# Eight heads' value products at once in the last cross attention, and an earlier normalisation in its feed-forward

## The chip, the cores and the metric

The kernel runs on one core of one Trainium2 chip. The metric is the device time of one execution in microseconds (us); the time before is the median of three runs, 4806.71 us (4796.98 to 4807.12). The core's engines run side by side, each in the order of its own instructions: TensorE (PE; its weight loads are listed as PEld), VectorE (DVE), ScalarE (ACT), GpSimd (POOL), and SyncE (SP), which issues the DMAs here. They wait for each other through semaphores. TensorE writes its results to PSUM, a small memory of banks; DVE and ACT bring them from there to SBUF, the working memory.

## What is computed

Four layers work on x, 32 samples of 112 rows by 256, with a context of 375 rows per sample:

```python
x = _L0_xattn_ref(x, ctx, ...)       # cross attention, 16 heads of 64
x = _L1_xattn_ref(x, ctx, ...)       # quantised self and cross attention, gated feed-forward
x = _L2_xattn_ref(x, ctx, ctx, ...)  # cross attention, feed-forward
x = _L3_xattn_ref(ctx, x, ...)       # self attention, cross attention, feed-forward
```

The change touches the second and third step of the last layer:

```python
h = _mha(_ln(x, ln2_g, ln2_b), x_e, cq_w, ..., causal=False)   # x_e is the context
x = x + h @ c_proj_w + c_proj_b
h = relu(_ln(x, ln3_g, ln3_b) @ f_w1 + f_b1) @ f_w2 + f_b2     # 256 -> 1024 -> 256
return x + h
```

`_mha` has 16 heads of 16: scores q·k over 375 context rows, softmax, times the values, heads side by side.

## The kernel before

**Sweeps.** The layers are cut into nine sweeps over the 32 samples: `l0x`, `l1s`, `l1x`, `l1f`, `l2x`, `l2f`, `l3s`, `l3x`, `l3f` (the digit is the layer; s is self attention, x cross attention, f feed-forward). Two sweeps often run interleaved. In the last stage these are `l3x` and `l3f`: `l3f` follows `l3x` by a few samples and takes x from it on chip (`beside`). The end of `l3s` lies beside the start of `l3x`.

**Units and slots.** A unit of `l3x` is one sample with eight slots, one for two heads (`pair`, in `unit16`). A unit of `l3f` is a pair of samples with eight slots, one for each 128 columns of the hidden layer (`unitff`). `order` lays the slots of all sweeps in one list by planned times (`SPAN`, `DELAY`); `run` goes through it. Each slot has up to five steps, and `LAGS` says how many slots of its own sweep later each step comes. For a slot of `l3x`:

- `a`, at once: the scores of both heads (L1166, PE, to PSUM tiles `sc`, of which there are three), the maximum (L640, DVE), the exponential with its sum (L646, ACT) into a `k3` tile in SBUF.
- `r`, one slot later: the reciprocal of the sum (L680, DVE) and the scaling (L219, POOL, two instructions).
- `b`, three slots later: three transposes for each head (L698, PE, to `ps` tiles), and their copies to another `k3` tile, one on ACT (L202), one on DVE (L204).
- `c`, four slots later, only in every second slot: `av`, the products with the values for the four heads of the last two slots (L1130, PE; 12 matmuls, which the profile shows as 24). Four heads are called a quad below. Eight heads share one PSUM tile, allocated with the first quad and moved to SBUF after the second, with the bias, by ACT (L224) or DVE (L228) and DVE (L1150).
- the last slot's fifth step: the output projection (L237 to L239, "ps<-w,ot") and the sum with x (L1267, DVE).

Every product that must keep float32 accuracy is made as three matmuls of high and low halves, L237, L238 and L239 (`mm3`). The halves are cut with a copy (L202, L204 or L206) and a subtraction (L233).

A slot of `l3f` makes an up projection (`up`, L237 to L239, "ps<-h,w"), the ReLU with bias on ACT (L224, "s<-ps"), the high half on ACT (L202, "ot<-s"), the low half on POOL or DVE (L233, "ot"), and one slot later the down projection into one PSUM tile for the unit (L237 to L239, "acc<-w,ot"). The bias goes into that tile first (L291).

**Buffers.** The tag `k3` has 11 buffers: softmax outputs, transposed probabilities, loaded values, and the projected queries of `l3x` ("k<-ps,vec_L_xattn_cq_b", L224 and L976) while they are stored to memory (dq_l3x) and read back in another layout. PSUM holds four tiles `ps`, three `sc` and one `acc`. A tile whose buffers are all in use waits for the last reader of one of them.

**Atoms.** What a unit needs beforehand are atoms: small functions with a lead, in slots of their sweep, before the unit's first slot (`LEAD`). For a layer norm (`norm_atoms`) these are `load`, `stats` (L460 to L462 on DVE, L435 on POOL) and `apply` (L475 on DVE and POOL, transposes L477 on PE, L213 or L215, L202/L204/L206 and L233). Projections are atoms too and are spread by `fill` over the slots.

**The order on the engines.** `run` gives an order of issue, which the framework's scheduler then changes by its own estimates and by priorities: `av` of the unquantised sweeps is issued within `high_priority(offset=400)`, which lets it move ahead.

Of the kernel before, what the change touches and what calls it, by code (L numbers as in the profile page):

```python
# [61 lines left out]
class Kern:  # L62
# [12 lines left out]
        l3x=[0, 1, 3, 4, 4],  # L75
        l3f=[0, 4, 1, 4, 3],
# [8 lines left out]
        l2f=dict(load=6, stats=5, apply=3),  # L85
        l3s=dict(load=10, stats=8, apply=7, q=7, qload=3, k=6, v=3, c2=7, k2=1, v2=1),
        l3x=dict(load=16, stats=11, apply=10, cload=13, cut=12, q=9, qload=4, k=8, v=6, kload=8, vload=4),
        l3f=dict(load=3, stats=3, apply=2),
    )

    EARLY = 4
    HORIZON = dict(l0x=8, l1s=8, l1x=11, l1f=11, l2x=16, l2f=1, l3s=19, l3x=14, l3f=9)
    PARTS = dict(l0x=3, l1s=3, l1x=3, l1f=6, l2x=3, l2f=3, l3s=2, l3x=1, l3f=4)
    SCTAG = dict(l1x=("ps1", "sc"), l3x=("sc", "sc"))
    TWICE = ()

    SHARE = {
        ("l0x", "copy"): (1, 0, 0), ("l0x", "xn"): (0, 1, 2), ("l0x", "ohi"): (0, 1, 0), ("l0x", "prob"): (0, 1, 7),
# [959 lines left out]
    def unit16(self, s, b0, i, gb, g, wd, quant, self_attn, qb, kb, vb, dl, gvec, bvec):  # L1058
# [56 lines left out]
        def av(heads, pt, first, octets, ahead=True):  # L1115

            if first:
                st["av"] = self.ps([128, 2, S])
            o = st["av"]

            turn = list(enumerate(heads))
            if ahead and nb > 1:
                turn = turn[2:] + turn[:2]
            with self.tc.high_priority(offset=400) if ahead else nullcontext():
                for a in range(nb):
                    for n, hd in turn:
                        r = hd % 4
                        oc = hd // 8 if both else 0
                        odd = hd // 4 % 2
                        nc.tensor.matmul(  # L1130
                            o[32 * r : 32 * r + 32, oc, :],
                            st["v"](a, hd),
                            pt(a, n),
                            start=a == 0 and odd == 0 and oc == 0,
                            stop=a == nb - 1 and odd == 1 and oc == both,
                            tile_position=(0, 32 * r),
                        )
            if octets:
                if octets[0] == 0:
                    st["ot"] = self.t([128, 2, 2, S], F32R, "ot")  # L1140
                oc = slice(octets[0], octets[-1] + 1)
                hi, lo = st["ot"][:, 0, oc, :], st["ot"][:, 1, oc, :]
                o = o[:, : len(octets), :]
                if quant:
                    self.scale("ohi", hi, o, dl["so"])
                    nc.vector.scalar_tensor_tensor(lo, o, dl["so"], hi.bitcast(F32), ALU.mult, ALU.subtract)
                else:
                    bi = vb[:, octets[0] : octets[0] + 1]
                    self.shift("ohi", hi, o, bi)
                    nc.vector.scalar_tensor_tensor(lo, o, bi, hi.bitcast(F32), ALU.add, ALU.subtract)  # L1150

        def pair(pr):
# [38 lines left out]
            def c():  # L1191
                if m == 0 or qd % 2 == 0 and s in self.TWICE:
                    return
                for qq in (qd - 1, qd) if s in self.TWICE else (qd,):
                    heads, ocs = range(4 * qq, 4 * qq + 4), [qq // 2] if qq % 2 else []
                    if quant:
                        with self.tc.issue_after(self.mark[s].ins):
                            av(heads, lambda a, r: st["pt", qq][: blocks[a][1], 3 * r + a, :], qq % 2 == 0, ocs, False)
                    else:
                        av(heads, lambda a, r: st["pt", qq, r // 2][:, r % 2, a * S : (a + 1) * S], qq % 2 == 0, ocs)  # L1200
# [3 lines left out]
        def quad(qd):  # L1204
# [39 lines left out]
            def c():  # L1244
# [5 lines left out]
                st["pt", qd] = pt  # L1250
                if qd % 2 == 0 and s in self.TWICE:
                    return
                for qq in (qd - 1, qd) if s in self.TWICE else (qd,):
                    av([8 * (qq // 2) + qq % 2 + 2 * i for i in range(4)], lambda a, n: st["pt", qq][:S, n, :], qq % 2 == 0, [qq // 2] if qq % 2 else [])
# [414 lines left out]
```

## Time and profile before

| what | value |
|---|---|
| median of three runs | 4806.71 us (4796.98 to 4807.12) |
| profiled execution, its own time | 4799.79 us |
| its span, first to last instruction | 4797.7 us |
| busy share of the span: PE, PEld, DVE, ACT, POOL | 93%, 83%, 75%, 71%, 44% |
| mean granted clock of PE | 0.968 |
| last stage: one pair of samples (`l3x` and `l3f`) | 44.85 us |
| first score of `l3x`; last value product of `l3x` | 3996.5 us; 4771.7 us |

The profile is one execution. A group of rows has a line of the code, an engine, what is written and read, a count and times. "Idle before" names what ended a wait. A granted clock of 1.00 is full speed of TensorE. Matmuls overlap, so their length is longer than the step from one to the next; steps are read from start times.

### The profile page before, as it was taken

To read this page: it belongs to the slowest core of one execution; us is meant where nothing else is said; L and a number is where in the kernel's file an instruction comes from. 1 tells how busy PE (TensorE), PEld (TensorE's weight loads), DVE (VectorE), ACT (ScalarE), POOL (GpSimd) and SP (SyncE) were. 2 spreads that over 40 slices of the span, in tenths; PEclk is the share of its full clock that TensorE was granted. 3 is DMA by queue.
4 is the path that set the end of the run, shared out by engine and by line. 5 is a ranking of instruction groups with operands and counts; after the bars stand their busy time and mean duration, and the time that the engine had idled before them with its cause. 6 is when DMAs were issued, how large, how long until landed. Compare 5 with 4: busy or idle time off the path is not lost.

```text
span 4797.7 us, 111165 instructions
## 1 busy us (share of the span) xinstructions
PE 4449.6 (93%) x37824; PEld 3960.6 (83%) x37824; DVE 3619.7 (75%) x9803; ACT 3412.9 (71%) x10645; POOL 2131.3 (44%) x3676
## 2 busy tenths in 40 slices
PE   7999999998778999999999999999999997899999
PEld 6888888887667888887999999998899986778888
DVE  5788888888888888887688888888566655677776
ACT  5788888887767777775577777775555554677776
POOL 5455455556444343333233333334444443566665
PEclk9999999999889999999999999999999997899999
DMA  4433333334665565566355445543777777666663
GB/s 109 125 87 88 82 86 82 83 84 120 139 132 136 147 144 147 145 153 160 108 144 144 138 140 140 146 142 103 198 218 220 221 201 207 159 165 166 164 166 84
DMA packets 590020, 674.50 MB, mean 141 GB/s; under 512 B 331488, under 2 KB 499664, under 8 KB 589264
## 3 DMA queue, kind: packets, MB, share of 16 engines
q1 hardware_dynamic: 589456, 667.38, 54.6%
q8 instruction: 305, 5.00, 0.5%
q14 instruction: 259, 2.12, 0.1%
HBM read 323.55 MB, written 173.02 MB: 104 GB/s over the span
## 4 chain that ended last, share of the span: by engine, by line
PE 42%; DVE 5%; DMA 4%; ACT 1%; issue 1%; POOL 1%; SPq 0%; ACTq 0%; DVEq 0%; POOLq 0%
PE ps L698 7%; PE ps L237 6%; PE ps L238 5%; PE ps L239 5%; PE sc L807 3%; PE ps L829 3%; PE ps L1130 3%; PE sc L1166 2%; PE acc L237 2%; PE acc L239 1%; PE acc L238 1%; PE ps L1294 1%; DVE sm L640 1%; PE ps L1240 1%; DMA k<-k 1%
## 5 line engine op out<-in xcount | busy, mean ns | idle before, releaser
L219 POOL TENSOR_SCALAR k<-k,sm 112x375 f32<-112x375 f32 (+1 forms) x1536 | 941.7, 626 | 1054.1 <-DVE sm L680 474.5
L202 ACT ACTIVATE k<-ps 125x336 f32<-125x336 f32 (+4 forms) x2005 | 916.3, 470 | 419.8 <-PE ps L239 185.2
L640 DVE TENSOR_REDUCE sm<-sc 112x1 f32<-112x375 f32 x1792 | 945.1, 539 | 150.7 <-PE sc L807 86.6
L646 ACT ACTIVATE k<-sc,sm 112x375 f32<-112x375 f32 x1536 | 881.9, 580 | 103.3 <-DVE sm L640 79.9
L698 PE MATMUL ps<-ident,k 112*125 112x112 f32 x4608 | 736.4, 278 | 20.4 <-issue 4.0
L698 PEld LDWEIGHTS ps<-ident,k 112*125 112x125 f32 x4608 | 653.5, 191 | 76.0 <-issue 45.7
L807 PE MATMUL sc<-k,qs 128*112 128x376 f32 x2048 | 540.7, 357 | 21.4 <-ACT k L646 11.4
L237 PE MATMUL ps<-w,k 128*125 128x256 f32 (+2 forms) x1344 | 426.3, 317 | 32.0 <-ACT k L646 17.4
L729 DVE TENSOR_TENSOR k<-ps,k 64x376 fp32r<-64x376 f32 x640 | 350.3, 547 | 121.7 <-ACT k L202 106.5
L237 PE MATMUL ps<-h,w 128*128 128x224 f32 x1408 | 408.8, 297 | 34.6 <-DVE h L204 13.0
L204 DVE COPY k<-ps 125x336 f32<-125x336 f32 (+2 forms) x619 | 289.7, 468 | 152.3 <-PE ps L239 60.2
L238 PE MATMUL ps<-h,w 128*128 128x224 f32 x1408 | 394.0, 282 | 2.6 <-POOL h L233 2.0
L239 PE MATMUL ps<-h,w 128*128 128x224 f32 x1408 | 393.2, 282 | 1.3 <-POOL w L233 1.2
L238 PE MATMUL ps<-w,k 128*125 128x256 f32 (+2 forms) x1344 | 385.6, 287 | 0.0
L239 PE MATMUL ps<-w,k 128*125 128x256 f32 (+2 forms) x1344 | 384.7, 286 | 0.0
L829 PE MATMUL ps<-k,k 125*64 125x112 f32 (+1 forms) x4608 | 351.9, 297 | 1.6 <-ACT k L202 1.3
L215 POOL TENSOR_SCALAR k<-k,sm 112x375 f32<-112x375 f32 x256 | 165.8, 648 | 416.8 <-DVE sm L680 314.9
L237 PE MATMUL ps<-k,w 128*128 128x376 f32 x896 | 336.5, 376 | 15.2 <-ACT k L646 5.8
L807 PEld LDWEIGHTS sc<-k,qs 128*112 128x112 f32 x2048 | 305.3, 177 | 50.7 <-ACT k L646 24.9
L237 PEld LDWEIGHTS ps<-w,k 128*125 128x125 f32 (+2 forms) x1344 | 258.8, 193 | 82.5 <-ACT k L646 30.3
L646 ACT ACTIVATION_READ_ACCUMULATOR k<-sc,sm 112x1 f32 x1536 | 323.7, 211 | 0.0
L237 PEld LDWEIGHTS ps<-h,w 128*128 128x128 f32 x1408 | 272.4, 197 | 56.8 <-issue 18.2
(216 smaller groups left out, 12559.6 us busy)
## 6 DMA issues: line engine op xcount, KB each, us to landing
qs<-h SPq DMA_DIRECT2D x512, 224.0 KB
k<-k SPq DMA_DIRECT2D x192, 376.0 KB
k<-cd SPq DMA_DIRECT2D x64, 752.0 KB
vd<-k SPq DMA_DIRECT2D x128, 375.0 KB
k<-vd SPq DMA_DIRECT2D x128, 375.0 KB
qs<-dq_l3s SPq DMA_DIRECT2D x128, 224.0 KB
qs<-dq_l3x SPq DMA_DIRECT2D x128, 224.0 KB
x<-xd SPq DMA_DIRECT2D x224, 112.0 KB
```

The source lines that it names most:

```text
L202: self.nc.scalar.activation(out, in_, AF.Identity)
L204: self.nc.vector.tensor_copy(out, in_)
L219: self.nc.gpsimd.tensor_scalar(out, in_, by, 1.0, ALU.mult, ALU.mult)
L237: mm(out, lhs(0), rhs(0), start=start, stop=False)
L238: mm(out, lhs(0), rhs(1), start=False, stop=False)
L239: mm(out, lhs(1), rhs(0), start=False, stop=stop)
L640: nc.vector.tensor_reduce(nms[j], sc[j][:, :n], AX.X, ALU.max, negate=True)
L646: nc.scalar.activation(p[:, j, :n], sc[j][:, :n], AF.Exp, bias=nms[j], scale=1.0 if scale is None else scale, accum_out=sm[:, j : j + 1])
L698: self.nc.tensor.transpose(pst[:TB, a * S : (a + 1) * S], p[:, j, a * TB : (a + 1) * TB], self.ident[:S, :S])
L729: nc.vector.tensor_tensor(ks[o, j, :], pk[r, :TE], ks[r, j, :].bitcast(F32), ALU.subtract)
L807: nc.tensor.matmul(sc[:, :TE], qs[:, hd, q, bs], kk, start=q == 0, stop=q == 1)
L829: nc.tensor.matmul(o if gqa else o[:, mm, :], vq[:, a, hd * 64 : hd * 64 + 64], st["pt"][:, :, j, ta] if gqa else st["pt", mm][:, j, ta], ...
```

## The change

Two class constants change. `TWICE` makes step `c` of `l3x` return in the slot of the first quad and issue both quads' products in the slot of the second, two slots (four heads) later; the PSUM tile for the eight heads is then allocated there as well, and the first quad's transposed probabilities are kept until then. `LEAD["l3f"]` puts loading, statistics and application of the feed-forward's layer norm one slot of `l3f` earlier. Nothing else changes; the same instructions are issued.

```diff
-        l3f=dict(load=3, stats=3, apply=2),
+        l3f=dict(load=4, stats=4, apply=3),
...
-    TWICE = ()
+    TWICE = ("l3x",)
```

The code that reads `TWICE`, in `pair` (not changed):

```python
            def c():
                if m == 0 or qd % 2 == 0 and s in self.TWICE:
                    return
                for qq in (qd - 1, qd) if s in self.TWICE else (qd,):
                    heads, ocs = range(4 * qq, 4 * qq + 4), [qq // 2] if qq % 2 else []
                    ...
                        av(heads, lambda a, r: st["pt", qq, r // 2][:, r % 2, a * S : (a + 1) * S], qq % 2 == 0, ocs)
```

## The prediction

> **What bounds the kernel now.** I read the busy shares by slice first. TensorE (PE) is busy 93% of the span; the last five slices of 120 us, where most of the change lies, hold 9 at full clock. DVE and ACT stay at 6 and 7 there.
>
> ```profile
> PE   7999999998778999999999999999999997899999
> ...
> PEclk9999999999889999999999999999999997899999
> ```
>
> Then the stretches of the last stage, one per pair of samples. Columns: stretch and length in us, busy time of PE, its weight loads, DVE, ACT and POOL, granted clock, DMA share, GB/s.
>
> ```profile
> 4369.00:4414.00 45.00, 41.65 (x478) 36.76 (x477) 34.16 (x101) 33.86 (x109) 28.02 (x44) 1.00 0.70 170
> 4414.00:4459.00 45.00, 42.13 (x449) 36.99 (x452) 32.95 (x97) 32.10 (x103) 29.61 (x45) 0.96 0.65 164
> ```
>
> The pattern repeats every 44.85 us (the stall below stands at 4423.30, 4468.67, 4513.05). PE idles some 3.2 us per pair, and in every second pair the clock is granted at 0.96. PE bounds the stage. So a gain must come from fewer or cheaper PE instructions or from less waiting, and a loss from more waiting.
>
> The waits of PE alone, 4150 to 4700 us (total us, times, longest):
>
> ```profile
> PE sc L1166 <- ACT k L646: 9.6, 27, 1.3
> PE acc L237 <- ACT ot L202: 8.0, 13, 0.6
> ...
> PE ps L1130 <- ACT k L202: 2.8, 3, 1.3
> ```
>
> The 13 in the second row are the 13 pairs: once per pair the feed-forward's down projection (acc, L237) waits 0.61 us for the ReLU chain. The timeline of PE shows why, and what switching to the value products (L1130) costs (start, length, then what):
>
> ```profile
> 4393.14 0.48 PE L698 MATMUL ps<-ident,k 112*125 112x112 f32 x3
> 4393.39 0.40 PE L1166 MATMUL sc<-k,qs 128*112 128x376 f32 x1
> 4393.63 0.48 PE L698 MATMUL ps<-ident,k 112*125 112x112 f32 x3
> 4394.04 0.78 PE L1130 MATMUL ps<-k,k 125*32 125x112 f32 x24
> 4394.75 0.43 PE L1166 MATMUL sc<-k,qs 128*112 128x376 f32 x1
> ...
> 4407.45 0.28 PE L239 MATMUL acc<-w,ot 128*112 128x256 f32 x1
> 4407.66 0.38 PE L1130 MATMUL ps<-k,k 125*32 125x112 f32 x2
> 4407.97 0.58 PE L698 MATMUL ps<-ident,k 112*125 112x112 f32 x3
> 4408.48 0.78 PE L1130 MATMUL ps<-k,k 125*32 125x112 f32 x22
> 4409.19 0.58 PE L698 MATMUL ps<-ident,k 112*125 112x112 f32 x3
> 4409.53 0.40 PE L1166 MATMUL sc<-k,qs 128*112 128x376 f32 x1
> ```
>
> Three transposes (L698) before a score (L1166) take 0.25 us from start to start; before value products 0.41. A group of 24 takes 0.71, the score after it 0.27 instead of 0.24. One group's way in and out costs 0.41 - 0.25 + 0.03 = 0.19 us. A group split around transposes is dearer: from 4407.57 (the L239 before it steps by 0.12) to 4409.53 are 1.96 us for 24 products and 6 transposes, against 0.71 + 0.25 + 0.25 = 1.21: 0.75 us of overhead.
>
> **The change, part by part.** The program does the same arithmetic; only the order moves. All of it lies after 4000 us. In the built order, one steady pair (12 of them) has, for its eight quads of heads: before, 10 or 11 groups of value products, 2 or 3 of them splits; after, 4 or 5 groups and no split.
>
> *Value products for eight heads.* Overhead before: 2.5 splits x 0.75 + 5.5 whole groups x 0.19 = 2.9 us. After: 4.5 x 0.19 = 0.85. PE saves 2.1 us a pair, 12 x 2.1 = 25 us. The run-in beside l3s goes from 45 to 30 groups, but PE is only 72% busy in 4000 to 4100 and waits for DMAs there, so I count 15 x 0.19 = 3 us at most and take 2; the last pairs have 8 groups fewer, about 2 us. Sum: -29 us, -4 of it outside the 12 pairs.
>
> *What the later products displace.* The early half of the products was what PE did between an up projection and the down projection that needs its ReLU. Cover is measured as PE time between the two in the built order, at the row lengths above. Before, one of eight has 0.49 us of cover (two scores) and the rest 1.3 us or more; the short one waits 0.61, so the chain needs 1.10 us:
>
> ```profile
> 4422.18 0.51 PE L1166 MATMUL sc<-k,qs 128*112 128x376 f32 x2
> 4423.30 0.37 PE L237 MATMUL acc<-w,ot 128*112 128x256 f32 x1 [0.61 <-ACT ot L202]
> ...
> 4430.00 0.41 PE L238 MATMUL ps<-h,w 128*128 128x224 f32 x1
> 4430.21 0.41 PE L239 MATMUL ps<-h,w 128*128 128x224 f32 x1
> ```
>
> After, three in a row are short, just after the query projection of the next pair: 0.49; 0.49 in eight pairs, 0.98 or 1.34 in four; 0.98 in eight, 0.49 to 0.73 in four. Filled up to 1.10, the two new ones wait 0.43 + 0.24 us on the mean. The low half also needs POOL (L233, 0.66 us, starting when ACT ends). In the old short case a score stands between; in the new ones mostly two matmuls of 0.11 each, leaving 0.66 - 0.22 + 0.05 (a semaphore's delay: ACT's L202 ends at 4423.25, PE starts at 4423.30) = 0.5 us, once and a half per pair. Together +1.4. The low end is 0, if the chain starts earlier than its order suggests; the high end 2 x (0.61 + 0.5) = 2.2.
>
> *Banks and buffers behind the query projection.* With the products gone from there, six transposes follow at once and wait for PSUM: the second set for ACT's copy, which is third on ACT (0.35 + 0.44 us after the first L224), the last set for the ReLU (0.45). I get 0.6 + 0.5 us. In the same place before, PE waits 1.27 (L1166 <- L646, at 4477.07) or 0.8 to 1.3 (L1130 <- L202), so this is 0, between -0.3 and +0.3. What is queued behind on ACT is the next softmax, priced next.
>
> *The probabilities kept longer.* Four transposed tiles now live until the eighth head's, in the same 11 k3 buffers. In the built order a softmax output (L646) now takes the buffer of the second half of the queries, and so waits for its store. That store is slow in one period:
>
> ```profile
> 4251.40 0.44 DVE L976 SCALAR_TENSOR_TENSOR k<-ps,vec_L_xattn_cq_b,k 128x224 fp32r<-128x224 f32 x1
> 4256.73 0.45 ACT L202 ACTIVATE k<-ps 125x336 f32<-125x336 f32 x1 [0.79 <-DMA dq_l3x<-k]
> ```
>
> From 4251.84 to 4256.73 are 4.9 us; in the pair at 4477 nothing waits for it. Before, a copy of the probabilities waited for it, and PE lost 0.3 (L698 <- L202). Behind the exponential on ACT's queue stand a copy, three more exponentials and the ReLU, and behind those PE's scores, for which only three banks exist. At 4.9 us ACT is stopped some 1.6 us longer, and PE loses as much. At the fast end the exponentials still stand behind the ReLU pair (0.45 + 0.39) with nothing else for PE to score: about 0.4. I take the middle, +1.0 a pair, between 0.4 and 1.6.
>
> *Clock.* Clusters of idle time are followed by half clock: after 4422 to 4429 (2.7 us idle) the same L237 matmuls step by 0.21 us instead of 0.11, for 3.4 us, costing 1.7. Other pairs, with 3.5 us idle but spread over 9, have none. The new waits stand directly behind this cluster. I take 0.6 of a dip more per pair; PE would wait anyway in some 30% of it, so 0.6 x 1.7 x 0.7 = +0.7, between 0 and 1.7. [...]
>
> *Feed-forward normalised one slot sooner.* Its transposes stand at 4400.15 and the unit's bias matmul at 4414.28; the up projection that reads the result comes no earlier than 4410. It is ahead already, so moving it by one slot (44.85 / 8 = 5.6 us) wins nothing. No DMA is added: the loads of x go through memory no more than before, as the pair hands x over on chip. On POOL it moves L435 and L475 (0.72 + 1.33 us) ahead of one softmax scaling (L219, 1.17); the transposes of that scaling come some 4 us later, which hides it. If that cover is gone: 2 us a pair, taken as 0.
>
> Sum per pair: -2.1 + 1.4 + 0 + 1.0 + 0.7 = +1.0, times 12 is +12. Outside the 12 pairs -4, and +2 for the run-in, whose built order shows the same short covers. In all +10 us. The profiled execution took 4799.79 us (span 4797.7), 6.9 below the median of 4806.71; two of three runs lie at 4807. So 4809.8 beside the profiled one, 4817 beside the median, +0.2%.
>
> **The rivals.** (1) *Faster: the switches count and the waits do not.* The saved issue time appears in any case, while each wait can shrink: ACT and DVE are idle 25% here. It decides where the added waits and dips stay below 2.1 us a pair. With half of them (1.55): -0.55 x 12 - 3 = -10, 4797; with none: -29, 4778. Against it: the short covers are plain in the order, and the 0.61 recurs 13 times unchanged.
> (2) *Same: they cancel.* No further dips and the store at its fast end: (-2.1 + 1.4 + 0.4) x 12 - 2 = -6; with the middle store +2: 4801 to 4809. For it: pairs with 3.5 us idle and no dip.
> (3) *Clearly slower: all at their upper ends*, -2.1 + 2.2 + 0.3 + 1.6 + 1.7 = +3.7, times 12 less 2 is +42: 4849. For it: the rows of 4256.73 and 4430.00. Against: most pairs do not show the slow store.
> (4) *The change does nothing.* For the products the order refutes it; for the feed-forward it is my forecast.
>
> **How the numbers follow.** Three runs of one kernel span 10 us, so 0.2% (9.6 us) is about what can be told from no change. Forecast, slower by 0.2 to 0.6%: 0.38. Rival 1: 0.29. Rival 2, within 0.2%: 0.22. Rival 3: 0.11. Slower altogether 0.49. The sum stands just at the edge between slower and same, so either sign is open; I give 4817. The range leaves out the lowest part of rival 1 and half of rival 3: 4783 to 4846. The forecast alone has 4816 to 4835.
>
> **What would show it.** Right: pairs longer than 44.85 us; the row L237 <- ACT ot L202 with two to three times 13 waits, and a new PE row waiting for POOL L233; groups of 48 L1130 and no split; more stretches with a clock of 0.96 or less. Wrong if pairs take 43 us or less with the waits near 3.2 us, or if PE waits chiefly for the feed-forward's normalisation, or for value loads.

## The result

The changed kernel takes 4827.08 us (median of 8 runs, 4818.45 to 4841.52) against 4805.51 us (median of 8 runs, 4796.98 to 4815.97): ratio 1.0050, 95% interval 1.0039 to 1.0061. It is 0.5% slower. The forecast was slower by 0.2 to 0.6%, and the time lies in the range. The sign and the size came out, but by luck: the experiments show that the loss came from a step that the prediction had costed at nothing, while the step that was to bring it cost nothing that can be told from no change.

First the profile after: the busy shares by slice, of which two of the last five hold 8 (9 throughout, before).

```profile
PE   7999999998779899999999999998999986898989
...
PEclk9999999999889999999999999999999997899999
```

The slices are too coarse for the clock. The stretches by pair of samples show more. Here each runs from one unit's bias matmul (L291, "acc<-biases") to the next; columns as in the prediction.

```profile
4344.72:4392.96 48.24, 41.88 (x457) 37.25 (x455) 34.45 (x99) 32.94 (x104) 28.27 (x45) 0.96 0.64 158
...
4673.86:4717.89 44.03, 39.19 (x453) 35.45 (x452) 34.05 (x98) 32.94 (x104) 27.24 (x44) 1.00 0.66 164
```

Pairs now take between 44.03 and 48.29 us. The three quickest, 44.03, 44.24 and 45.01 us, are those at full clock throughout. The waits of PE in the same stretch as before, 4150 to 4700 us:

```profile
PE sc L1166 <- ACT k L646: 17.3, 28, 2.2
PE acc L237 <- ACT ot L202: 9.9, 18, 0.6
...
PE ps L237 <- DVE k L976: 5.2, 6, 0.9
...
PE acc L239 <- POOL ot L233: 3.2, 13, 0.3
```

Scores (L1166) wait 17.3 us for the exponential instead of 9.6. The down projection waits 18 times for L202 instead of 13, and 13 times for the low half (L233), which is new. New is also the query projection's second half, waiting for the first half's halves (L976). The products themselves did what the change says. In this line of PE's timeline 48 of them stand together:

```profile
4387.24 1.36 PE L1130 MATMUL ps<-k,k 125*32 125x112 f32 x48
```

And the store of the queries holds up the softmax, as forecast. PE's timeline first, then ACT's in the same place:

```profile
4361.97 0.91 PE L698 MATMUL ps<-ident,k 112*125 112x112 f32 x6 [0.41 <-DVE k L976]
4364.92 0.98 PE L1166 MATMUL sc<-k,qs 128*112 128x376 f32 x2 [2.04 <-ACT k L646]
```

```profile
4361.60 0.45 ACT L224 ACTIVATE s<-ps,vec_L_xattn_f_b 128x224 f32<-128x224 f32 x1 [0.17 <-PE ps L239]
4364.20 0.57 ACT L646 ACTIVATE k<-sc,sm 112x375 f32<-112x375 f32 x1 [2.15 <-DMA dq_l3x<-k]
```

ACT stands 2.15 us before an exponential whose output tile is still being stored as queries; behind it PE stands 2.04 us before a score.

**An account of the steady pairs.** For the rest of the document each profile's 12 steady pairs are split into three: waits (the sum of PE's waits in its timeline), half clock (time at a granted clock of 0.50, halved, since L237 to L239 "ps<-h,w" then step by 0.21 us instead of 0.11, as at 4429.57 us and 4429.09 us of the kernel before; an upper bound, as part of it falls into waits), and the remainder, which is issue time. "Windows" counts stretches of 3.41 us at half clock. All per pair, in us:

| kernel | pair | waits | half clock (windows in 12 pairs) | remainder |
|---|---|---|---|---|
| before | 44.83 | 3.22 | 0.71 (5) | 40.90 |
| changed | 46.38 | 4.93 | 1.71 (12) | 39.74 |
| e1: merged products only | 44.75 | 4.34 | 0.43 (3) | 39.98 |
| e2: earlier norm only | 46.61 | 3.60 | 1.28 (9) | 41.72 |
| e3: changed, queries in pp2 | 44.64 | 3.97 | 1.99 (14) | 38.68 |
| e4: e1, queries in pp2 | 43.33 | 2.96 | 1.14 (8) | 39.22 |
| e5: changed, matmuls before the wait | 46.59 | 4.41 | 1.56 (11) | 40.62 |
| e6: before, queries in pp2 | 44.29 | 2.28 | 0.43 (3) | 41.58 |
| e7: changed, matmuls in the wait | 45.63 | 4.19 | 0.71 (5) | 40.73 |
| e8: changed, application back | 45.55 | 4.81 | 1.14 (8) | 39.61 |
| e9: e4, earlier query projection | 41.68 | 2.18 | 0.43 (3) | 39.08 |
| e10: e4, matmuls in the wait | 43.33 | 2.70 | 0.57 (4) | 40.06 |
| e11: e6, earlier norm | 46.08 | 2.70 | 1.28 (9) | 42.10 |
| e12: changed, statistics back | 47.50 | 4.68 | 2.56 (18) | 40.26 |

The change adds 1.55 us a pair: waits +1.7, half clock +1.0, issue -1.2. Times 12 that is 18.6 us. Outside the pairs, the run-in beside l3s takes 246.0 us instead of 238.4 and the end 66.3 instead of 69.0. The two spans differ by 32.5 us, 8.9 of which lie ahead of the run-in. There single profiles differ anyway: the bias matmul near 3860 us, ahead of all that the edits move, stands between 3857.2 and 3873.7 in these profiles. So pairs are compared by profile, and kernels by the timed ratio.

### The profile page after: what moved, and what is told of

The parts are those of the page before. It is cut to its first block, busy times and chain, and to the rows that moved or that the text cites. A ratio compares the mean times of both kernels' runs of the same rounds, so it can differ in the third digit from the quotient of the medians.

```text
span 4830.2 us, 111200 instructions
## 1 busy us (share of the span) xinstructions
PE 4446.1 (92%) x37824; PEld 3969.9 (82%) x37824; DVE 3625.9 (75%) x9803; ACT 3415.7 (71%) x10645; POOL 2113.3 (44%) x3676
## 5 line engine op out<-in xcount | busy, mean ns | idle before, releaser
L219 POOL TENSOR_SCALAR k<-k,sm 112x375 f32<-112x375 f32 (+1 forms) x1536 | 931.7, 619 | 1063.8 <-DVE sm L680 486.4
L202 ACT ACTIVATE k<-ps 125x336 f32<-125x336 f32 (+4 forms) x2005 | 913.3, 468 | 424.9 <-PE ps L239 178.7
L646 ACT ACTIVATE k<-sc,sm 112x375 f32<-112x375 f32 x1536 | 878.2, 577 | 119.2 <-DVE sm L640 70.4
L698 PE MATMUL ps<-ident,k 112*125 112x112 f32 x4608 | 725.4, 277 | 27.8 <-DVE k L976 4.6
L237 PE MATMUL ps<-w,k 128*125 128x256 f32 (+2 forms) x1344 | 427.5, 318 | 30.3 <-ACT k L646 16.4
L237 PE MATMUL ps<-h,w 128*128 128x224 f32 x1408 | 408.4, 297 | 40.4 <-DVE h L204 12.8
L239 PE MATMUL ps<-h,w 128*128 128x224 f32 x1408 | 393.8, 282 | 1.3 <-POOL w L233 1.2
L239 PE MATMUL ps<-w,k 128*125 128x256 f32 (+2 forms) x1344 | 385.7, 287 | 0.0
L237 PE MATMUL ps<-k,w 128*128 128x376 f32 x896 | 336.2, 375 | 16.4 <-ACT k L646 5.9
L215 POOL TENSOR_SCALAR k<-k,sm 112x375 f32<-112x375 f32 x256 | 165.0, 645 | 417.1 <-DVE sm L680 315.5
L237 PEld LDWEIGHTS ps<-w,k 128*125 128x125 f32 (+2 forms) x1344 | 260.1, 194 | 83.9 <-ACT k L646 30.0
L237 PEld LDWEIGHTS ps<-h,w 128*128 128x128 f32 x1408 | 273.6, 198 | 61.0 <-issue 16.8
L646 ACT ACTIVATION_READ_ACCUMULATOR k<-sc,sm 112x1 f32 x1536 | 319.6, 208 | 0.0
```

Source lines behind the costliest of these rows:

```text
L202: self.nc.scalar.activation(out, in_, AF.Identity)
L219: self.nc.gpsimd.tensor_scalar(out, in_, by, 1.0, ALU.mult, ALU.mult)
L237: mm(out, lhs(0), rhs(0), start=start, stop=False)
L239: mm(out, lhs(1), rhs(0), start=False, stop=stop)
L646: nc.scalar.activation(p[:, j, :n], sc[j][:, :n], AF.Exp, bias=nms[j], scale=1.0 if scale is None else scale, accum_out=sm[:, j : j + 1])
L698: self.nc.tensor.transpose(pst[:TB, a * S : (a + 1) * S], p[:, j, a * TB : (a + 1) * TB], self.ident[:S, :S])
```

## The experiments

The first four kernels ran together on one chip (before: median 4801.76 us). All kernels compute the whole result; e5, e7 and e10 do more matmuls than needed.

**The two halves of the change.** e1 is the changed kernel with the old lead, e2 the kernel before with the new one:

```diff
# e1, against the changed kernel
-        l3f=dict(load=4, stats=4, apply=3),
+        l3f=dict(load=3, stats=3, apply=2),
# e2, against the kernel before
-        l3f=dict(load=3, stats=3, apply=2),
+        l3f=dict(load=4, stats=4, apply=3),
```

> Products for eight heads at once, the feed-forward's normalisation left where it was. Theory A (the loss comes from the merged products: per pair 1.7 us less issue time, but 1.7 us more waiting and 1 us more half clock): about the time of the change, 4820 to 4832 us, pairs of 46 to 46.7 us. Theory B (the earlier normalisation does the harm, by its place in the queues): 4785 to 4800 us.

> Normalisation one slot sooner, products for four heads as before. Theory A: no change, 4800 to 4811 us, pairs of 44.6 to 45.1 us, since the normalisation was some 10 us ahead already. Theory B: slower, 4815 to 4830 us.

Measured: e1 4805.12 us, ratio 1.0005 (0.9995 to 1.0016); e2 4823.16 us, ratio 1.0045 (1.0030 to 1.0061). Theory A fell in both; theory B held in e2, while its range for e1, a gain, was missed too. The merged products alone cost nothing that can be told from no change, and the normalisation, which I had put at zero, costs all of it. The waits of PE in e1's 12 pairs (4207.56 to 4744.52 us):

```profile
PE sc L1166 <- ACT k L646: 12.7, 25, 1.1
PE acc L237 <- ACT ot L202: 8.4, 15, 0.6
...
PE ps L237 <- DVE k L976: 5.2, 6, 0.9
```

Waits rise by 1.1 us a pair, issue falls by 0.9, half clock falls by 0.3: they cancel, as rival 2 of the prediction had it. In e2 the products for four heads are split more often: groups of 2 next to 22 come 44 times in 12 pairs instead of 28. At the prediction's 0.75 us a split, 16 x 0.75 / 12 = 1.0 us a pair, which answers to the +0.8 in the remainder. Beside it come four more windows at half clock (+0.6) and waits (+0.4). The cover between the fifth up projection of a unit and its down projection (PE's work between the two, from its rows) falls from 2.6 to 3.2 us to 0.3 to 1.0 us. With merged products the norm's price is made up otherwise. From e1 to the changed kernel no group is split; the pair grows by 1.63 us, of which 1.28 are half clock, 0.59 waits and -0.24 issue. The fifth cover falls there too, from 2.3 to 2.6 us to 0.3 to 1.0. The softmax scaling on POOL, behind which the prediction hid the norm's POOL work, shows no sign of being the cause: no row of PE waits for it (L219) in the 12 pairs of the kernel before, e1, e2 or the changed one. What of this each of the norm's steps brings is asked below.

**The tiles that the stored queries hold.** In e3 the halves of the projected queries go to the tag pp2, whose four buffers of the same size l3s needs and l3x does not:

```diff
# e3, against the changed kernel; e6, against the kernel before; in qk_atoms.half
-                z["hl", c] = hl = self.t([128, 2, W], F32R, "k3")
+                z["hl", c] = hl = self.t([128, 2, W], F32R, "pp2" if isq and self.cur == "l3x" else "k3")
# e4: this edit, and the old lead of l3f
```

> The changed kernel, with the halves of the projected queries of l3x in tiles of another tag (pp2, four buffers, which the last stage hardly uses after l3s), so that no softmax output waits for their store. Theory A (the store holds up the softmax, as predicted, +1.0 us a pair, of which the profile of the change shows 0.6): ACT's rows L646 and L202 waiting for the DMA dq_l3x (9.5 us in 12 pairs) go, PE's L1166 waiting for L646 falls from 17 to 10 us in 12 pairs, and the time falls by 6 to 12 us, to 4815 to 4821. Theory C (the softmax is late for other reasons, the store is only the last of several): the wait changes its name, and the time stays at 4824 to 4830.

Measured: 4793.04 us, ratio 0.9981 (0.9970 to 0.9991). The expected direction, but three to six times the expected size: 34 us less than the changed kernel. ACT no longer waits for dq_l3x at all, and PE's waits for L976 are gone too. A new wait takes part of it back: in e3's 12 pairs,

```profile
PE sc L1166 <- DMA qs<-dq_l3x: 16.8, 7, 4.1
```

the queries are read back late, by 3.3 to 5.2 us in four pairs. Two more kernels (before: 4802.94 us) ask whether that and the gain belong to the tiles alone.

> Products for eight heads, the normalisation left where it was, and the halves of the queries in the pp2 tiles. Theory E (the earlier normalisation costs some 20 us with merged products, and the queries' tiles win some 30 us, each by itself): 4801.8 + 3 - 30 = 4770 to 4785 us, pairs of 42 to 43.5 us. Rival (with the queries' tiles free, the reads of the queries come late in every second pair, as in the run before, 3.3 to 5.2 us each, whatever the normalisation): 4788 to 4798 us, with PE's L1166 waiting some 17 us for the DMA qs<-dq_l3x in 12 pairs.

> The kernel before with the halves of the queries in the pp2 tiles. Theory A (with products for four heads nothing is kept that long, and the store holds up little: ACT waits 6.9 us for it in 12 pairs, of which PE loses 0.3): 4797 to 4804 us. Rival (the tiles win as much without the merged products, so that they and not the merging are what counts): 4770 to 4785 us.

Measured: e4 4782.68 us, ratio 0.9955 (0.9940 to 0.9970); e6 4800.89 us, ratio 1.0000 (0.9990 to 1.0010). So theory E and theory A held. The tiles win nothing with products for four heads, and make the merged products worth 0.45% where these were worth nothing. PE's waits in e4 (4186.25 to 4706.16 us) have no row for L976 and none for a DMA:

```profile
PE sc L1166 <- ACT k L646: 10.5, 24, 0.9
PE acc L237 <- ACT ot L202: 9.7, 20, 0.6
PE acc L239 <- DVE ot L233: 4.5, 6, 0.8
```

The remainder between e6 and e4 falls by 2.4 us a pair, near the 2.1 that the prediction took for the switches. But e6 has 40 split groups in 12 pairs where the kernel before has 28; against that kernel the remainder of e4 falls by 1.7. The gain was there, and with the shared k3 tiles it had been eaten. By which way is shown in part: from e1 to e4 the waits that name L976 go (7.6 us in 12 pairs, 0.6 a pair), but the order on PE changes too, and the remainder falls by 0.8.

**The cube closed.**

> The kernel before with the queries in pp2 tiles and the normalisation one slot sooner; it closes the cube of the three edits. Theory F (the earlier normalisation harms through the order on PE: more groups of products and short covers): 4816 to 4828 us, as without pp2. Rival (it harms through the tiles held by the store of the queries, which pp2 frees): 4798 to 4808 us.

e11 is e2 with the queries in pp2 (before: 4802.44 us). Measured: 4816.30 us, ratio 1.0030 (1.0019 to 1.0041), just over the lower end of theory F. The earlier norm costs in all four settings:

| ratio to before | old lead of the norm | one slot sooner |
|---|---|---|
| four heads | 1 | 1.0045 |
| eight heads | 1.0005 | 1.0050 |
| four heads, queries in pp2 | 1.0000 | 1.0030 |
| eight heads, queries in pp2 | 0.9955 | 0.9981 |

**Which part of the norm.** e8 and e12 put one step of it back each:

```diff
# e8, against the changed kernel
-        l3f=dict(load=4, stats=4, apply=3),
+        l3f=dict(load=4, stats=4, apply=2),
# e12, against the changed kernel
-        l3f=dict(load=4, stats=4, apply=3),
+        l3f=dict(load=4, stats=3, apply=3),
```

> The changed kernel with the application of the norm (L475, transposes L477) back at its old slot, loading and statistics one slot sooner. In the built order it differs little from the changed kernel: the same short covers. Theory F (the statistics' earlier place is what moves the order): as the change, 4820 to 4831 us. Rival (the application does it): as with the merged products alone, 4800 to 4810 us.

> The changed kernel with the statistics back at their old place, loading and application one slot sooner; in the built order the fifth up projection of a unit has its long cover back (1.7 us and more, against 0.49 to 0.98 in the changed kernel). Theory G (the harm of the earlier normalisation is this one short cover and the half-clock windows behind it): PE's acc L237 waiting for L202 falls from 18 to 15 times in 12 pairs, the half-clock windows from 12 to 6 or fewer, the time to 4803 to 4812 us. Rival (the application's transposes and their place among the value products do it, whatever the cover): 4818 to 4830 us.

Measured: e8 4815.93 us, ratio 1.0027 (1.0018 to 1.0036), between the two expectations; e12 4845.19 us beside 4797.04, ratio 1.0099 (1.0082 to 1.0117), beyond both. In e12 the short cover went as planned (the fifth is 1.6 to 2.0 us; L237 waits for L202 16 times, 8.0 us in its 12 pairs), but another wait took its place, with statistics and application now in the same slot:

```profile
PE ps L477 <- DVE xh L475: 16.4, 12, 1.5
```

So the time that theory G gave was missed, but with 1.4 us of new wait a pair e12 does not test the cover by itself. The waits say more: from e1 to the changed kernel all waits of the down projection grow by 0.9 us in 12 pairs, while the pairs grow by 19.6. Whether the half clock behind the short cover belongs to it stays open. What the profiles of the kernels with any earlier step of the norm share are 8 to 18 half-clock windows in 12 pairs (5 in e7, below, with six matmuls more a pair), against 3 to 8 without. A profile is one execution; the granted clock of all timed runs, a mean over the whole span, bears it out in three settings (0.9650 in the changed kernel against 0.9674 in e1, 0.9667 in e2 against 0.9677 before, 0.9657 in e3 against 0.9672 in e4) and not in the fourth (0.9671 in e11, 0.9670 in e6). Which instruction of the norm displaces what stays open; each edit changes the built order in many places at once.

**The clock.** e5 and e7 put extra matmuls into the pocket before the query projection, to see whether half clock follows from idle PE:

```diff
# e5, against the changed kernel, in qk_atoms.half, before the projection's matmuls
+            for n in range(8 if isq and c == 0 and self.cur == "l3x" else 0):
+                nc.tensor.matmul(pq, w()[:, 0, 0, :128], self.biases[:, :W], start=True, stop=True)
# e7, against the changed kernel, at the end of norm_apply
+        for n in range(6 if self.cur == "l3x" else 0):
+            nc.tensor.matmul(pst[:, n % 2, :], self.biases[:, :128], self.biases[:, :W], start=True, stop=True)
```

> The changed kernel, with eight more matmuls of 224 columns per pair of samples (results overwritten by the first real one), put before the query projection, where PE waits 1.0 to 1.4 us for the normalised x. Theory D (half clock follows a window of 3.41 us in which PE was idle more than about 1.2 us, so filling the wait prevents it): of the 12 windows at half clock in the last 560 us at most 6 are left, the time falls by 6 x 1.7 = 10 us or more, to 4812 to 4818. Rival (the clock has other causes, or the fillers come too late to lie in the wait): the windows stay, and the time is 4827, or up to 14 us more (16 x 8 x 0.11).

> The changed kernel with six more matmuls of 224 columns per pair of samples, into the bank of the normalised x after it has been read, so that they can only run while PE waits for the halves of it (L202, L204, L206). Theory D (half clock follows windows of 3.41 us with over about 1.1 us of idle PE, in the runs so far 43 of 98 such and none of 820 with less): the wait of 1.0 to 1.4 us is filled by 0.66, the half-clock windows in 12 pairs fall from 12 to 6 or fewer, and the time by 6 to 12 us, to 4815 to 4821. Rival (idle PE is not the cause): the windows stay and the time is 4827 to 4835 us.

e5: 4833.76 us, ratio 1.0064 (1.0049 to 1.0079), 11 windows left, as its rival had it. It says nothing on the clock, since the matmuls missed the wait: the scheduler put them between the two transposes of the norm (at 4404.11, the second transpose at 4405.07), so the norm came later and the wait stayed at 1.02 to 1.21 us. e7's can start only when L215 has read the bank. The changed kernel first, from the norm's second transpose (L477) to the projection, then e7:

```profile
4355.72 0.41 PE L477 MATMUL ps<-ident,xh 112*128 112x112 f32 x2 [0.22 <-POOL xh L475]
4357.34 0.37 PE L237 MATMUL ps<-h,w 128*128 128x224 f32 x1 [1.21 <-DVE h L204]
```

```profile
4350.70 0.41 PE L477 MATMUL ps<-ident,xh 112*128 112x112 f32 x2 [0.22 <-POOL xh L475]
4352.13 0.93 PE L495 MATMUL ps<-biases 128*128 128x224 f32 x6 [1.02 <-DVE xh L215]
4352.90 0.27 PE L237 MATMUL ps<-h,w 128*128 128x224 f32 x1
```

They do not fill the wait either: PE still idles 1.02 to 1.25 us before them (1.03 to 1.43 before the projection in the changed kernel), and the projection starts 0.75 us later after the transposes, on the mean of 12 pairs. What went down is the scores' waiting for the exponential behind it, from 17.0 to 9.7 us in 12 pairs. e7: 4820.48 us, ratio 1.0036 (1.0022 to 1.0051); 5 windows instead of 12, as theory D expected. The idle time is spread wider: full-clock windows with more than 1.3 us of idle PE fall from 9 to 1. So this fits theory D without showing that filling a wait prevents half clock. The intervals of e7 and the changed kernel overlap, so the 7 us are likely rather than certain; the windows are counted in one execution each. The same on e4 (before: 4802.44 us):

> As the run with merged products, old normalisation and the queries in pp2 tiles, and six more matmuls in the wait for the halves of the normalised x. Theory D (idle PE sets the clock): of the 8 windows at half clock in 12 pairs at most 3 are left, 5 x 1.7 = 8 us, and the extra matmuls cost 2 to 3 us net, as they did on the changed kernel: 4774 to 4780 us. Rival: the extra matmuls take as much as the clock gives, 4781 to 4787 us.

e10: 4782.33 us, ratio 0.9964 (0.9952 to 0.9977): no gain over e4. Windows fell from 8 to 4 rather than 3, and the six matmuls added 0.8 us of issue time a pair, as much as waits and clock gave back. The rival held.

**A version that beats both.** e9 is e4 with

```diff
-        l3x=dict(load=16, stats=11, apply=10, cload=13, cut=12, q=9, ...),
+        l3x=dict(load=16, stats=12, apply=11, cload=13, cut=12, q=10, ...),
```

> As the run with merged products, old normalisation and the queries in pp2 tiles, and the query projection of l3x with its norm (statistics, application, projection) one slot of l3x sooner. Theory: the built order has no short cover (under 1.4 us) between up and down projection left in that place, so the 14 us that PE waits in 12 pairs for L202 and L233 of the ReLU fall to under 4, and the time to 4770 to 4778 us. Rival (the queries are stored earlier, but the norm now comes before the x it needs, or collides with the value products): 4783 to 4795 us.

Measured: 4767.74 us, ratio 0.9933 (0.9920 to 0.9946); below the range expected, 35 us under the kernel before. In its 12 pairs (4194.89 to 4695.10 us):

```profile
PE sc L1166 <- ACT k L646: 11.4, 24, 0.6
...
PE acc L239 <- DVE ot L233: 3.1, 6, 0.5
PE acc L237 <- ACT ot L202: 2.5, 9, 0.3
```

The ReLU waits fall from 14.2 us to 5.6 (expected: under 4), and three windows at half clock are left.

## Why the prediction was right, and where it was not

The sum said +1.0 us a pair, measured were +1.55; the time lies 10 us above the one given. Step by step, before to changed:

- *Feed-forward normalised one slot sooner: 0.* **This is the step that failed.** Measured alone, it is +0.45%, some 21 us. The argument was that the norm is early enough already, so moving it wins nothing, and that its POOL work hides behind a softmax scaling. The second part held, as no PE row waits for that scaling. But both looked for what the step gains or directly delays. What came with it is another order on PE: with four heads 16 more split groups in 12 pairs, with and without merging a short fifth cover and, in the profiles, more windows at half clock. In the change itself it is mostly half clock (+1.28 of 1.63 us a pair). The prediction saw the short cover in the built order (its third in a row is the fifth of a unit, and e1 does not have it), but I compared only the order of the whole change with that before, and put every difference down to the merged products. How the earlier norm brings the half clock is not shown.
- *Value products: -2.1.* Near it where nothing hides it (-2.4 from e6 to e4, whose base has 12 splits more; -1.7 from the kernel before to e4); -1.2 in the change's own remainder, -0.9 in e1.
- *Probabilities kept longer: +1.0.* Right mechanism and place. Too small: the waits for L646 show +0.6 (9.3 to 16.9 us in 12 pairs), but taking the cause away made pairs 1.4 us shorter (e1 to e4) and 1.7 (changed to e3), with the waits for L976 and others behind it.
- *Banks behind the query projection: 0.* Too small. Waits that name L976 rise from 1.7 to 7.5 us, +0.5 a pair; with the queries in pp2 they vanish (e3, e4), which speaks for the k3 tiles and not for PSUM.
- *Short ReLU covers: +1.4.* Too large: all waits of the down projection go from 7.4 to 12.5 us, +0.4 a pair. L237 waits 18 times, not the two to three times 13 that were named as the sign, and the waits at L233 are 0.25 us, not 0.5.
- *Clock: +0.7.* Measured +1.0 (7 more windows x 1.7 / 12). But in e1 it is -0.3, so in these profiles it came with the norm and not, as I argued, with the merged products' waits.
- *Outside the pairs: -2.* Measured +7.7 in the run-in and -2.7 at the end, +5. In the run-in scores wait 21.4 us for the exponential instead of 14.5; e1 has the same (+7.2); with the freed tiles e3 has none (238.3 us), but e4 +3.6.

Taken by itself, the merging was forecast to lose 10 us and lost 2.4 (0.05%, interval -2.4 to +7.7 us): rival 2. The merged products' terms (-2.1, +1.4, +1.0, +0.7) cancel within the measurement in e1. The norm then added what I had given to them, so the total came near by two errors that made up for each other. Rival 4, "the change does nothing", held in no part: for the feed-forward it was my forecast and it was wrong.

## What to carry to other kernels

Price each constant of a change by itself, and build the order for each: a step that "is early enough already" can still change the order of other work, and here moving it was the whole loss. Merging work to save switches lengthens the life of its inputs; look up what else shares their buffers before counting the saving, since here it was eaten until the stored queries got tiles of their own (0.9955 instead of 1.0005). And look at waits that stand close together: in the changed kernel three of 0.26, 0.45 and 0.47 us within 3.41 us stood ahead of 3.41 us at half clock, which cost up to 1.7 us beyond their own 1.18.

## What was not expected of the hardware

In these profiles half clock came in whole steps on one grid. The five stretches in the kernel before begin at 4337.32, 4429.48, 4525.05, 4606.97 and 4699.13 us, whose distances are 27, 28, 24 and 27 times 3.4133 us to within 0.02; each lasts 3.41. In its run-in, between 4016.46 and 4142.76 us, others last 6.83, 10.24, 13.65 or 17.07 us. The three grid windows around one of them in the changed kernel, with the granted clock third from the end:

```profile
4363.78:4367.19 3.41, 2.13 (x37) 1.38 (x41) 1.62 (x4) 2.98 (x11) 1.41 (x3) 1.00 0.28 50
4367.19:4370.60 3.41, 3.41 (x36) 3.08 (x28) 1.19 (x4) 2.22 (x7) 0.69 (x2) 0.50 0.99 222
4370.60:4374.01 3.41, 2.54 (x17) 1.99 (x17) 2.71 (x10) 2.06 (x6) 2.28 (x5) 1.00 1.07 218
```

PE is busy for 2.13 of 3.41 us in the first, so idle for 1.28, and the next window runs at half clock. Over the steady pairs of all 14 profiles (windows laid on the starts of the half-clock stretches, idle time from PE's rows), of windows at full clock with under 1.1 us of idle PE 3 of 1893 were followed by one at half clock; with 1.1 to 1.3 us 35 of 132; with more 52 of 65. The idle time was not always one gap: ahead of the half clock at 4421.81 us in the changed kernel it was three, of 0.26, 0.45 and 0.47 us. No single gap in the pairs of the kernel before and the changed one exceeds 2.3 us. As an estimate from these counts, a wait's price jumps: 0.2 us more takes a window that holds 1.0 from the first group (3 of 1893) to the second (35 of 132), and a window of 3.41 us at half clock costs up to 1.7.
